# One output product of a graph network on one core: three float32r products of split operands in place of one float32 product

## The chip, the core and the metric

The kernel runs on one core of one Trainium2 chip. Its time is the device time of one execution in microseconds (us). Five engines work side by side: TensorE (PE in the profile, with PEld for its weight loads) multiplies matrices into the accumulation banks (PSUM), VectorE (DVE), ScalarE (ACT) and GpSimd (POOL) work element by element, and SyncE (SP) issues the DMAs. Each engine takes its instructions in the order in which the program put them, and waits for semaphores of the others.

## The reference

There are 128 independent graphs of 128 nodes with 256 features. Layer 0 normalizes, applies a gated graph network of three rounds (a product with a weight, a product with the adjacency matrix, a GRU cell) and adds the result to its input. Layer 1 normalizes again and applies graph attention:

```
h   = max(layernorm(x), 0)
Wh  = h W^T                               # 128 x 256 for each graph
e   = leaky_relu(s1[i] + s2[j]),  s1 = Wh a1,  s2 = Wh a2
att = softmax(e, masked by the adjacency matrix)
out = x + att Wh
```

All is float32.

## The kernel before

Four graphs make a group, and there are 32 groups (`NG`), numbered 0 to 31. A planner written in Python (class `Order`) decides, while the program is built, in which order each engine gets its instructions: every step is a generator that yields (engine, estimated length, earliest start), and the planner issues the step that can start first, with ranks that break near ties. The order is fixed in the program after that.

Layer 0 runs one round of one group at a time on TensorE and interleaves the rounds of neighbouring groups. The last round of group 30 is followed by that of group 31, which alone is done in two halves of two graphs each. Layer 1 of a group is the generator `epilogue`, started when the group's third round is done. For the last two groups it stays on the core, with no way round over DRAM. Its steps are, with the lines of the profile:

- TensorE turns the state to rows (`pr_o`, L527); DVE adds it to the input (L967), takes the statistics (L440 to L449) and POOL the inverse root; ACT normalizes (`h_b`, L471)
- DVE makes the two score columns of each graph (L998, into `s`)
- TensorE puts the mask and the turned score in a bank (`ps`, L1009 and L1016); ACT adds the other score and applies the leaky unit (`e`, L1046)
- DVE takes the row maximum (L1061, into `soft`), ACT the exponential with its sum (L1065)
- TensorE transposes the result (`pp`, L1074), ACT copies it to `prT` (L1078, or L1083 in group 31 with the scale of the normalization); DVE makes the inverse of the sum and the row scale `rs` (L1093, L1095)
- TensorE gathers the neighbours, `h` times `prT` (L637, into two banks `pq`); ACT, and for the second bank in group 31 DVE, copy them to `hs` (L1116), 128 x 1024 for the four graphs, with the features on the partitions
- TensorE makes the output product `hs` times `gwt`, the transposed weight, 128 x 256 for each graph and two products of 128 rows each (L1124); DVE multiplies it by `rs` and adds it to the rows (L1132)
- SyncE stores the rows (L60): 512 KB for a whole group, or in group 31 128 KB for each graph.

In the trace's names a bank appears as `po`, `pp`, `ps` or `pq` where it comes from the pool of three, and as `u`, `m` or `c` where, in the last stretch, one of the five banks of layer 0 is used in its place. `xt` is the tile of rows of groups 29, 30 and 31.

Of the kernel before, what the change touches and what calls it, by code (L numbers as in the profile page):

```python
# [7 lines left out]

F32 = mybir.dt.float32
I32 = mybir.dt.int32  # L10
AF = mybir.ActivationFunctionType
ALU = mybir.AluOpType
AX = mybir.AxisListType

P = 128
D = 256
C = D // P
G = 4
# [3 lines left out]
EPS = 1e-5  # L22
ALPHA = 0.2
BIG = 1e30


@with_exitstack
def preln_gnn_kernel(
# [14 lines left out]
    nc = tc.nc  # L43
    B = x.shape[0]
    NG = B // G
# [11 lines left out]
    put = on_pe  # L57
# [19 lines left out]
    small = ctx.enter_context(tc.tile_pool(name="small", bufs=4))  # L77
# [52 lines left out]
    gwt = const.tile([P, C, D], F32, name="gwt")  # L130
# [13 lines left out]
    for bank in (*c1, c2):  # L144
        bank = bank.rearrange("p g t -> p (g t)")
# [19 lines left out]
    PE, ACT, DVE, DVE2, POOL, SP = "PE", "ACT", "DVE", "DVE2", "POOL", "SP"  # L165
# [146 lines left out]
    order = Order()  # L312
# [627 lines left out]
    def epilogue(s, hT, graphs, ready):  # L940

        g = s.g
# [3 lines left out]
        name = f"{g}_{graphs[0]}"  # L946
        bank_t, row_t, graph_t = 0.57 * n / G + 0.02, 0.62 * n / G + 0.02, 0.11 * n

        late, h = g >= NG - 3, None
# [3 lines left out]
        if late:  # L953
            banks, ready = yield from to_rows(hT, ready, f"{name}_o", graphs)
        else:
            h, ready = yield from to_rows_by_blocks(hT, ready, f"b{name}")
            s.kept.append(h)
            if g < NG - XT:
                yield from load_x1(s)
                ready = max(ready, s.x1_ready)  # L960
        x1 = s.x1
        for i, two in enumerate(twos(graphs)):
            t = yield (DVE if late else DVE2), 0.31 * len(two), ready
# [8 lines left out]
        if final_one:  # L972

            rstd, nb, t, t2 = yield from norm_scales(x1, graphs, t - HOP, f"b{name}", True)
        else:
            rstd, nb, t = yield from norm_scales(x1, graphs, t - HOP, f"b{name}")
        h, t = yield from norm_apply(
            x1, graphs, None if final_one else rstd, nb, t, f"b{name}", s.kept,
            "tq" if end else "h",
        )  # L980
        if final_one:
            t = max(t, t2)
# [3 lines left out]
        ready = t  # L986
        place = min(part.start, G - 2)
        for i in (1, 0):
            for k in graphs:
                first = not late and s.prT is None  # L990
                t = yield (DVE2, 0.53, ready, "prT") if first else (DVE2, 0.53, ready)
# [12 lines left out]
        if late:  # L1004
            t = yield PE, 4 * graph_t if end else graph_t, max(t, s.off_ready), "misc"
            p2 = order.open("misc", f"ps2_{name}")
            if end:
# [3 lines left out]
                    start=True, stop=False, skip_group_check=True,  # L1011
                ))
            for k in graphs:
                turned = p2[:, k * P : (k + 1) * P]
                if end:
                    put(nc.tensor.matmul(  # L1016
                        turned, two[:, k : k + 1].to_broadcast([P, P]), ident,
                        start=False, stop=True, skip_group_check=True,
# [3 lines left out]
        else:  # L1022

            t = yield DVE, 0.1, t - HOP
            turned = score_tiles[g % 2]
            put(nc.vector.transpose(turned, turned))
            ready, line = t, None
            for q in range(Q):
                t = yield SP, 0.45, ready
# [4 lines left out]
            t = yield SP, 0.45, t + LAND, "e"  # L1034
            s.e = order.open("e", f"e_{g}")
            dma(s.e, line.rearrange("(o k) p -> o k p", o=1).to_broadcast([P, G, P]))
            t = t + 2.5
            t = t + LAND
        ready = t
        for k in graphs:  # L1040
            t = yield (ACT, 0.4, ready, e_room) if s.e is None else (ACT, 0.4, ready)
            if s.e is None:
                s.e = place_of_e(g)
            e = s.e
# [7 lines left out]
        if not end:  # L1052
            off_ready = yield from mask(s, ready)
            t = yield DVE2, row_t, max(t, off_ready) - HOP
# [3 lines left out]
        t = yield DVE, row_t, t - HOP  # L1058
        soft = small.tile([P, 4, G], F32, tag="soft", name=f"soft_{name}")
        nm, total, inv, rs = (soft[:, i, :] for i in range(4))  # L1060
        put(nc.vector.tensor_reduce(nm[:, part], le, AX.X, ALU.max, negate=True))  # L1061
        ready = t
        for k in graphs:
            t = yield ACT, 0.5, ready
# [4 lines left out]
        ready = t  # L1069
        if late:  # L1070
            t = yield PE, graph_t, t, "misc"
# [3 lines left out]
            prT = s.prT  # L1075
            if not final_one:
                t = yield ACT, bank_t, t
                put(nc.scalar.copy(prT[:, part, :].rearrange("p k s -> p (k s)"), pp[:, cols]))  # L1078
            else:
                ready = t  # L1080
                for k in graphs:
                    t = yield ACT, 0.3, ready
                    put(nc.scalar.activation(  # L1083
                        prT[:, k, :], pp[:, k * P : (k + 1) * P], AF.Identity,
                        scale=rstd[:, k : k + 1],
                    ))
            order.close(f"pp_{name}", t)
        else:
            t = yield from squares_by_blocks(e, s.prT, t, str(g))
            prT = e  # L1090
# [8 lines left out]
        banks, ready = yield from gathered(h, prT, t, f"pq_{name}", graphs)  # L1099
# [5 lines left out]
        for c, pq in enumerate(banks):  # L1105
            on = DVE if c and final_one else ACT
            t = yield (on, bank_t, ready, hs_room) if s.hs is None else (on, bank_t, ready)
            order.close(f"pq_{name}_{c}", t)
            if s.hs is None and end:
                hs = work.tile([P, 4, H], F32, tag="ta", name=f"hs_{g}")  # L1110
# [3 lines left out]
            hs = s.hs  # L1114
            copy = nc.vector.tensor_copy if on == DVE else nc.scalar.copy
            put(copy(hs[:, c, cols], pq[:, cols]))  # L1116
        ready = t

        for ks in twos(graphs) if not final_one else [range(k, k + 1) for k in graphs]:
            t = yield PE, 0.865 * len(ks), ready, "misc"  # L1120
            po = order.open("misc", f"po_{g}_{ks[0]}").rearrange("p (k d) -> p k d", d=D)
            for j, k in enumerate(ks):
                for c in range(C):
                    put(nc.tensor.matmul(  # L1124
                        po[:, j, :], hs[:, c, k * P : (k + 1) * P], gwt[:, c, :],
                        start=(c == 0), stop=(c == C - 1),
                    ))
            if final and ks[-1] == graphs[-1] and not end:
                order.close(f"hs_{g}", t)
            for j, k in enumerate(ks):  # L1130
                t2 = yield DVE, 0.4, t
                put(nc.vector.scalar_tensor_tensor(  # L1132
                    x1[:, k, :], po[:, j, :], rs[:, k : k + 1], x1[:, k, :], ALU.mult, ALU.add
                ))
            order.close(f"po_{g}_{ks[0]}", t2)
            if final_one:
                yield SP, 0.45, t2
                dma(out[g * G + k], x1[:, k, :])
        if final_one:
            return  # L1140
        t = yield SP, 0.45, t2
        ks = slice(g * G + part.start, g * G + part.stop)
# [92 lines left out]
    for slot, (g, l) in enumerate(plan):  # L1235
        s = groups[g]
# [53 lines left out]
```

## Time and profile before

| what | value |
|---|---|
| time, median of 3 runs | 2126.38 us (2125.87 to 2126.73) |
| profiled execution, first to last instruction | 2124.5 us; the profile gives no other time for it |
| granted TensorE clock over the span | 1.000 |
| TensorE busy | 2116.6 us, 10865 matmuls |
| VectorE busy | 1733.1 us |
| ScalarE busy | 1301.4 us |
| GpSimd busy | 126.5 us |
| DMA | 211.95 MB, 100 GB/s on the mean |

In the profile's rows a name such as `L1124 PE MATMUL po<-gwt,hs` is the line of the kernel, the engine, the operation and what it writes and reads. A float32 product is two matmul records. Rows of the timeline and of the chain of waits begin with the start in us from the first instruction and the length in us; `x8` are eight instructions taken together, and `[0.61 <-ACT e L1046]` says how long the engine was idle before it and what ended that. In rows of groups, busy us and the mean ns of one stand between the bars, and the idle time before them after the second bar.

### The profile page before, as it was taken

The numbers are of one execution on the slowest core, as the hardware profiler recorded it, in microseconds if no ns is written. First come the engines' busy times: TensorE is split into PE (matmuls) and PEld (weight loads), VectorE is DVE, ScalarE is ACT, GpSimd is POOL, SyncE is SP. The second block draws the span as 40 slices with busy tenths as digits, with TensorE's granted clock in tenths as the row PEclk, the third lists the DMA queues.
The fourth block names the chain that finished last, engine by engine and source line by source line (L and its number), as shares of the span: only waits on it lengthen the run. The fifth ranks groups of instructions, "written<-read, shape, count | busy, mean of one in ns | idle before, by whom it ended". The sixth has DMA issues, their size and how long they took to land.

```text
span 2124.5 us, 32340 instructions
## 1 busy us (share of the span) xinstructions
PE 2116.6 (100%) x10865; PEld 1886.8 (89%) x10865; DVE 1733.1 (82%) x3771; ACT 1301.4 (61%) x2875; POOL 126.5 (6%) x200
## 2 busy tenths in 40 slices
PE   9999999999999999999999999999999999999999
PEld 7888888888888888888888888888888888888888
DVE  7778888888878888888888888888888888787777
ACT  5556666566656666666656666666666566665666
POOL 1000000000000000000000000000000000000000
PEclk9999999999999999999999999999999999999999
DMA  5334454554455444545344554445453544444311
GB/s 159 65 85 88 86 118 107 107 117 92 98 115 119 84 96 107 122 109 113 83 108 104 117 122 82 98 106 123 110 107 88 107 107 105 96 98 94 70 31 46
DMA packets 667975, 211.95 MB, mean 100 GB/s; under 512 B 578336, under 2 KB 644640, under 8 KB 667808
## 3 DMA queue, kind: packets, MB, share of 16 engines
q1 hardware_dynamic: 667808, 209.87, 44.3%
q8 instruction: 86, 1.41, 0.3%
q14 instruction: 81, 0.66, 0.1%
HBM read 121.91 MB, written 87.88 MB: 99 GB/s over the span
## 4 chain that ended last, share of the span: by engine, by line
PE 98%; DVE 1%; ACT 0%; DMA 0%; issue 0%; POOL 0%; SPq 0%; ACTq 0%; DVEq 0%
PE c L737 35%; PE u L737 35%; PE m L737 12%; PE pa L637 8%; PE po L1124 5%; PE pq L637 2%; PE pw L378 0%; DMA xt<-in_x 0%; PE c L1124 0%; PE u L1124 0%; ACT v L688 0%; PE c L637 0%; PE pr_o L527 0%; DVE st_a L440 0%; PE pr L527 0%; ACT e L1065 0%
## 5 line engine op out<-in xcount | busy, mean ns | idle before, releaser
L830 ACT ACTIVATE z<-c,brz 128x256 f32<-128x256 f32 (+1 forms) x388 | 186.2, 480 | 328.4 <-PE c L737 186.4
L737 PE MATMUL u<-t_h,s_hh 128*128 128x256 f32 (+1 forms) x1164 | 345.0, 378 | 0.9 <-DVE c L763 0.5
L737 PE MATMUL u<-t_a,s_f 128*128 128x256 f32 (+1 forms) x1164 | 312.3, 377 | 0.0
L737 PE MATMUL c<-aT,s_f 128*128 128x256 f32 (+1 forms) x1164 | 312.3, 377 | 0.0
L795 ACT ACTIVATE r<-c,brz 128x256 f32<-128x256 f32 (+1 forms) x388 | 175.3, 475 | 194.3 <-PE c L737 112.8
L763 DVE TENSOR_TENSOR c<-u,m 128x512 f32<-128x512 f32 (+1 forms) x194 | 134.6, 694 | 140.8 <-PE u L737 140.4
L737 PEld LDWEIGHTS u<-t_h,s_hh 128*128 128x128 f32 x1164 | 218.4, 190 | 31.3 <-ACT c L757 1.6
L737 PEld LDWEIGHTS c<-aT,s_f 128*128 128x128 f32 x1164 | 220.4, 190 | 28.9
L737 PEld LDWEIGHTS u<-t_a,s_f 128*128 128x128 f32 x1164 | 220.4, 190 | 29.0
L737 PE MATMUL c<-hT,s_hh 128*128 128x256 f32 (+1 forms) x780 | 229.8, 376 | 0.0
L837 DVE TENSOR_TENSOR v<-v,c 128x256 f32<-128x256 f32 (+1 forms) x388 | 153.6, 415 | 66.3 <-PE c L737 43.7
L770 ACT COPY c<-u 128x512 f32<-128x512 f32 (+1 forms) x194 | 109.7, 566 | 117.5 <-PE u L737 116.1
L760 ACT COPY m<-m 128x512 f32<-128x512 f32 (+1 forms) x194 | 112.7, 581 | 107.1 <-PE m L737 106.9
L802 ACT ACTIVATE v<-c,bhn 128x256 f32<-128x256 f32 (+1 forms) x388 | 173.0, 474 | 0.0
L737 PE MATMUL m<-t_h,s_hh 128*128 128x256 f32 (+1 forms) x582 | 172.3, 378 | 0.0
L737 PE MATMUL c<-t_h,s_hh 128*128 128x256 f32 (+1 forms) x582 | 172.1, 377 | 0.0
L737 PEld LDWEIGHTS c<-hT,s_hh 128*128 128x128 f32 x780 | 147.6, 190 | 19.2
L774 DVE TENSOR_TENSOR c<-u,m 128x512 f32<-128x512 f32 (+1 forms) x194 | 131.8, 679 | 37.9 <-ACT c L770 34.9
L737 PE MATMUL u<-aT,s_f 128*128 128x256 f32 (+1 forms) x582 | 156.2, 377 | 0.0
L737 PE MATMUL m<-t_a,s_f 128*128 128x256 f32 (+1 forms) x582 | 156.1, 377 | 0.0
L737 PE MATMUL c<-t_a,s_f 128*128 128x256 f32 (+1 forms) x582 | 156.1, 377 | 0.0
L757 ACT COPY c<-u 128x512 f32<-128x512 f32 (+1 forms) x194 | 109.8, 566 | 43.7 <-PE u L737 43.7
(164 smaller groups left out, 3928.4 us busy)
## 6 DMA issues: line engine op xcount, KB each, us to landing
z<-tq SPq DMA_DIRECT2D x248, 128.0 KB
h<-z SPq DMA_DIRECT2D x248, 128.0 KB
xt<-in_x SPq DMA_DIRECT2D x31, 512.0 KB
z_a<-tq_a SPq DMA_DIRECT2D x120, 128.0 KB
hT_a<-z_a SPq DMA_DIRECT2D x120, 128.0 KB
z_b<-tq_b SPq DMA_DIRECT2D x116, 128.0 KB
h_b<-z_b SPq DMA_DIRECT2D x116, 128.0 KB
x<-in_x SPq DMA_DIRECT2D x29, 512.0 KB
```

The costliest lines, as they stand in the source:

```text
L637: put(nc.tensor.matmul(pa[:, k * P : (k + 1) * P], h[:, k, c * P : (c + 1) * P], A[:, k, :], start=True, stop=True,))
L737: put(nc.tensor.matmul(to(q), S[0][:, gate_no, weight, :], moving, start=first and q == 0 and i == 0, stop=(i == len(ends) - 1), skip_grou ...
L757: put(nc.scalar.copy(c1[0][:, :, 0:W], u[:, :, 0:W]))
L760: put(nc.scalar.copy(m[:, :, 0:W], m7[:, :, 0:W]))
L763: put(nc.vector.tensor_tensor(c2[:, :, 0:W], u[:, :, 0:W], m[:, :, 0:W], ALU.add))
L770: put(nc.scalar.copy(c1[1][:, :, 0:W], u[:, :, 0:W]))
L774: put(nc.vector.tensor_tensor(c22[:, :, 0:W], u[:, :, 0:W], m[:, :, 0:W], ALU.add))
L795: put(nc.scalar.activation(r[:, o, cols], src, AF.Tanh, bias=brz[:, o : o + 1], scale=0.5))
L802: put(nc.scalar.activation(v[:, o, cols], src, AF.Identity, bias=bhn[:, o : o + 1], scale=0.5))
L830: put(nc.scalar.activation(z[:, o, cols], src, AF.Tanh, bias=brz[:, C + o : C + o + 1], scale=0.5))
L837: put(nc.vector.tensor_tensor(v[:, o, cols], v[:, o, cols], src, ALU.add))
L1124: put(nc.tensor.matmul(po[:, j, :], hs[:, c, k * P : (k + 1) * P], gwt[:, c, :], start=(c == 0), stop=(c == C - 1),))
```

## The change

For group 30 alone (`g == NG - 2`) the output product is made otherwise. The operand `hs` is split into a part `hi` (ACT, `hs` times a factor just below one, written as float32r), the rest `lo` (DVE, `hs - hi`) and a combination `dif` (DVE). The weight `gwt` is split in the same way into `ghi` (ACT), `glo` and `gdif` (DVE, three steps). These six take three buffers of the pool `h`, two of `prT` and one of `e`. The product is then hi times ghi plus lo times glo in one bank, and dif times gdif in a second bank; each is multiplied by its own row scale (`rs_more`, `rs`) and added to the rows, so that there are two adds for each graph. The steps of the planner after that, the store among them, are unchanged.

```diff
+        halves = None
+        if g == NG - 2:
+            planes = []
+            t = ready
+            for i in range(3):
+                t = yield DVE, 0.1, t, "h"
+                planes.append(order.open("h", f"po_{g}_{i}").rearrange("p g d -> p (g d)").rearrange("p (c t) -> p c t", c=C).bitcast(F32R))
+            hi, lo, dif = planes
+            t = yield ACT, 1.2, t
+            put(nc.scalar.activation(hi, hs, AF.Copy, scale=BELOW))
+            t = yield DVE2, 1.22, t
+            put(nc.vector.tensor_tensor(lo, hs, hi.bitcast(F32), ALU.subtract))
+            t = yield DVE2, 1.22, t
+            put(nc.vector.scalar_tensor_tensor(dif, lo.bitcast(F32), -1.0 / UNIT, hi.bitcast(F32), ALU.mult, ALU.add))
+            ready = t
+            wides = []
...
+            t = yield ACT, 0.7, t
+            put(nc.scalar.activation(ghi, gwt, AF.Copy, scale=BELOW))
+            t = yield DVE2, 0.7, t
+            put(nc.vector.tensor_tensor(gdif, gwt, ghi.bitcast(F32), ALU.subtract))
+            t = yield DVE, 0.4, t
+            put(nc.vector.tensor_scalar(glo, gdif.bitcast(F32), 1.0 / UNIT, None, ALU.mult))
+            t = yield DVE2, 0.7, t
+            put(nc.vector.scalar_tensor_tensor(gdif, ghi.bitcast(F32), -UNIT, gdif.bitcast(F32), ALU.mult, ALU.add))
+            t = yield DVE, 0.1, t
+            rs_more = small.tile([P, 4, G], F32, tag="soft", name=f"more_{g}")[:, 0, :]
+            put(nc.vector.tensor_scalar(rs_more, rs, 1.0 + UNIT, None, ALU.mult))
+            halves = (hi, ghi), (lo, glo), (dif, gdif)
+            ready = max(ready, t)
...
+            if halves is not None:
+                for j, k in enumerate(ks):
+                    for c in range(C):
+                        for X, W in halves[:2]:
+                            put(nc.tensor.matmul(
+                                po[:, j, :], X[:, c, k * P : (k + 1) * P], W[:, c, :],
+                                start=(c == 0 and X is halves[0][0]), stop=(c == C - 1 and X is halves[1][0]),
+                            ))
+                t = yield PE, 0.5, t, "misc"
+                po2 = order.open("misc", f"po2_{g}_{ks[0]}").rearrange("p (k d) -> p k d", d=D)
+                X, W = halves[2]
+                for j, k in enumerate(ks):
+                    for c in range(C):
+                        put(nc.tensor.matmul(
+                            po2[:, j, :], X[:, c, k * P : (k + 1) * P], W[:, c, :],
+                            start=(c == 0), stop=(c == C - 1),
+                        ))
+                for j, k in enumerate(ks):
+                    for bank, scales_ in ((po, rs_more), (po2, rs)):
+                        t2 = yield DVE, 0.4, t
+                        put(nc.vector.scalar_tensor_tensor(
+                            x1[:, k, :], bank[:, j, :], scales_[:, k : k + 1], x1[:, k, :], ALU.mult, ALU.add
+                        ))
...
+                continue
```

The constants are `BELOW = 1 - 2^-13` and `UNIT = 2^-12`.

## The prediction

> **What bounds the kernel now.** The page first: TensorE is busy throughout and is 98% of the chain of waits.
>
> ```profile
> span 2124.5 us, 32340 instructions
> ...
> PE 98%; DVE 1%; ACT 0%; DMA 0%; issue 0%; POOL 0%; SPq 0%; ACTq 0%; DVEq 0%
> ```
>
> The change touches group 30 alone (NG is 32). Comparing the two built programs engine by engine, every queue is the same up to some 12 us before the end; what differs is the tail, so only the tail is priced. Second view: the chain of waits in order of time, from 2105 us on.
>
> ```profile
> 2111.06 1.73 PE po L1124 x8
> 2112.78 0.22 PE pp L1074 x2
> ...
> 2113.88 1.73 PE u L1124 x8
> 2115.61 0.45 PE m L637 x4
> ...
> 2117.72 0.89 PE pq L637 x8
> ...
> 2120.34 0.88 PE m L1124 x4
> 2121.22 0.02 issue
> 2121.24 0.48 DVE xt L1132
> ```
>
> `po` at 2111.06 and `u` at 2113.88 are group 30's output product: 16 matmul records in 3.46 us, each float32 product of 256 columns being two records 0.216 us apart. They stand between steps of group 31's softmax (`pp` transposes, `m` and `pq` gather), whose last add ends at 2121.72. Third view: the timeline of the tail, for what the other engines do there.
>
> ```profile
> 2112.35 9.74 SPq L60 DMA_DIRECT2D out<-xt  x6
> ...
> 2113.10 0.62 ACT L1083 ACTIVATE prT<-pp,norm_b 128x128 f32<-128x128 f32 x2 [1.75 <-PE pp L1074]
> 2113.92 0.62 ACT L1046 ACTIVATE e<-ps,s 128x128 f32<-128x128 f32 x2 [0.20 <-PE ps L1016]
> 2114.57 0.42 DVE L1061 TENSOR_REDUCE soft<-e 128x2 f32<-128x256 f32 x1 [0.61 <-ACT e L1046]
> 2115.03 0.40 ACT L1065 ACTIVATE e<-e,soft 128x128 f32<-128x128 f32 x1 [0.49 <-DVE soft L1061]
> ...
> 2121.24 0.48 DVE L1132 SCALAR_TENSOR_TENSOR xt<-m,soft,xt 128x256 f32<-128x256 f32 x1 [0.38 <-PE m L1124]
> ```
>
> The row to keep in mind is the maximum `L1061` of group 31's second half: it starts the moment its scores `e` are there, ACT's exponentials start 0.46 us later, and all that follows hangs on it: 7.15 us from its start (2114.57) to the last add's end (2121.72). Fourth view: the groups by form, VectorE (DVE) and ScalarE (ACT), for the prices.
>
> ```profile
> L694 DVE TENSOR_TENSOR hT<-hT,v 128x1024 f32<-128x1024 f32 x7 | 8.5, 1221 | 4.1 <-ACT v L688 4.1
> L698 DVE SCALAR_TENSOR_TENSOR hT<-hT,v 128x1024 f32<-128x1024 f32 x9 | 10.9, 1216 | 0.1
> L1055 DVE TENSOR_TENSOR e<-e,A 128x512 f32<-128x512 f32 x4 | 2.8, 690 | 0.2
> L930 DVE TENSOR_SCALAR A<-A 128x512 f32<-128x512 f32 x6 | 2.5, 415 | 0.0
> L1132 DVE SCALAR_TENSOR_TENSOR xt<-u,soft,xt 128x256 f32<-128x256 f32 x3 | 1.4, 480 | 1.0 <-PE u L1124 1.0
> L688 ACT ACTIVATE v<-v,bih 128x512 f32<-128x512 f32 x8 | 5.3, 715 | 0.0
> ```
>
> **The change, part by part.** The sum is made on this execution: span 2124.5 us; the median of the runs, 2126.38, is 1.88 us more, carried over unchanged.
>
> *Removed.* 16 records x 0.216 = 3.46 us of PE in front of group 31. `pp` then waits only for ACT's second exponential, whose accumulator is read by 2111.35, so `prT` runs at 2111.85 instead of 2113.10: 1.25 us earlier.
>
> *First split, on ACT and DVE.* In the new queues ACT's `hi` (128x1024) stands right behind `prT`: 715 ns for 512 columns, 499 ns for 256 (same line), so 0.22 us per 256 and 1.15 us for 1024: 2112.40 to 2113.55. Behind it wait `e` of group 31's second half and an `hs` copy; `e` is complete at 2114.36, against 2114.54 before, so the head start is spent. On DVE the queue is: `lo` (1.22 us, waiting for `hi`) to 2114.8, group 31's `hs` copy (0.42) to 2115.15, `dif` (1.22) to 2116.3, one add (pitch 0.40), then `L1061`. It starts at 2116.60 where it stood at 2114.57: **2.03 us later**, though its input was ready at 2114.36. This wait is the first cost, and PE and ACT idle for it.
>
> *From there to group 31's last add.* The chain of 7.15 us repeats with small shifts. On ACT `ghi` (0.71) comes between the exponentials and `prT` while PE transposes: 0.1 late. On DVE `gdif`, `glo` and `gdif` again (0.69 + 0.42 + 0.69) stand ahead of the last `hs` copy, which waits 0.44 us for them (ready 2120.0, done 2120.86). On PE eight float32r matmuls stand between group 31's last two products. Walked through with the rows, the `hs` copy ends 4.26 us after the maximum instead of 4.50 (PE's queue is emptier), and the last add 2.92 us after that instead of 2.65 (the eight matmuls, 0.89, less a product that is done by then): 2123.78, 7.18 us after the maximum. So **+0.03**.
>
> *The adds of group 30* now come last in DVE's queue: eight of 128x256 where there were four in the middle. Two independent ones together take 0.88 us in the timeline (at 2112.82), so 0.40 apart; dependent steps stand their duration plus 0.05 apart (`hT` at 2088.63, 2089.38 and 2090.11, 0.69 to 0.72 long), so 0.53; with four dependent pairs they end 3.75 us after group 31's last: **+3.75**. PE is ahead of them by then: at 0.111 us per float32r matmul its last is done at 2125.
>
> *The last transfer.* SyncE's queue now ends with group 30's 512 KB instead of 128 KB of group 31. The issue at 2112.35 (third view) has moved its 512 KB by 2114.93; the last 128 KB issue, at 2121.75, by 2123.10. That is 2.58 against 1.35 us: **+1.24**, with nothing left to hide it. The four 128 KB stores move ahead of it into an idle queue at no cost.
>
> *Pace of float32r.* No row has one. The built program has one matmul instruction for each (24 in place of 16). Low end: 0.111 us, two records of 128 columns (`pq`, 8 in 0.89 us). High end: 0.433, a whole float32 product. Between them, 0.216: the same columns at a float32 record's pace. I take 0.111, by the row that is nearest in kind, another type with one record to a product: the three bfloat16 products at the start (L146) pass 512 columns in about 0.42 us, where float32 records pass 256 in 0.426 in the same stretch, so such a record is twice as fast. 0.216 is kept as a rival.
> The Trainium skill, "FP8 and Floating Point Precision" (TensorE Precision Notes), says that true float32 takes four passes through the array, and reduced-precision float32 is read and truncated. By that one pass would be an estimated 0.433/4 = 0.108 us, and the sum the same within 0.05 us; the two records per product agree with multiple passes but do not show four.
>
> Sum: 2.03 + 0.03 + 3.75 + 1.24 = 7.05, so a span of 2131.5 and a time of **2133.4 us** (+0.33%).
>
> *Bounds of the rest.* `hi`: 0.99 (from copies, 586 and 372 ns) to 1.43 (twice 715): -0.16 to +0.28. The splits on DVE, writing float32r: at the rate of the `L930` row 0.8 us each for `lo` and `dif`, -1.2 with the weight's part, of which only the 0.44 us of waiting lies on the path; `glo` at 0.69 instead of 0.42: +0.27. Adds: all at 0.40, -0.5; all at 0.53 with a wait, +0.5. I take the rows of the same shape; the ends stay in the range. Planes and weights go into buffers whose readers were done over 10 us before (group 29's `e` is transposed at 2084), and opening them issues nothing: no cost, and if such a wait existed it would lengthen the first split one to one.
>
> *A rule against the change.* In the tail PE will have holes of up to 1.6 us (2113.6 to 2115.2, 2116.6 to 2118). This trace shows the granted clock at 1.00 to the end, also where PE is busy only 3.14 of 4.00 us (2104 to 2108); at the very start 256-column float32 records were 0.426 us apart instead of 0.216. I take full pace.
> "TensorE: Matmul & The Clock Gate" (The HAM clock gate) says that about 3.4 us of idleness halve the clock. No hole is that long; if the sparse stretch counted, rival 2's second case would hold.
>
> **Rivals.**
> 1. *float32r at the pace of a float32 record, 0.216 us.* The eight matmuls in front of group 31's last product take 1.73 instead of 0.89: +0.84; the last four records of group 30 then end at 2127.5 and its adds wait 0.6 us for them. 2134.9 us. For: every float32 record of 256 columns here takes that, and float32r has as many bytes. Against: float32's records come in pairs, and the bfloat16 row.
> 2. *The product is no cheaper than float32, 0.433 us, or the clock falls.* PE ends at 2132.6 and three adds follow: span 2138.2, time 2140.1; or, at half pace as in the start-up row, the 3.3 us of matmuls on the path after 2117 (`pp` 0.22, `pq` 0.89, products 1.30, eight float32r 0.89) double: 2136.7. For: nothing in the tail's rows. Against: the granted clock above.
> 3. *Not slower: the maximum is not held.* Group 31 comes forward by the PE time taken away. With no split in front of it `L1061` would start 0.8 us after `prT`, at 2113.25, 3.35 us before my 2116.60, and the sum fall to +3.7: 2130.1, within 0.2% of before. It decides where the maximum starts by 2113.8: `hi`, `lo`, the copy, `dif` and one add, 4.4 us by the rows, would have to take 1.6. Against: their order is fixed by the program, and three of them have rows over 1.1 us. Faster would need the eight adds and the 512 KB to be hidden as well, and nothing comes after them.
>
> **How the numbers follow.** Forecast (one pass, maximum held) 0.62; rival 1 0.2; rival 2 0.1; rival 3 0.05; something else 0.03. 0.2% of the time, 4.3 us, is about what a measurement of this kernel can tell from no change. All but rival 3 lie above 2130.6; slower 0.94, same 0.04, faster 0.02. Range: the low bounds together (-0.16 - 1.2 - 0.5) give 2131.5, and half a us of the way to rival 3 2131.0; the high ones (+0.28 + 0.27 + 0.5) on rival 1 give 2136.0, with part of rival 2 2137.0.
>
> **What would show it.** `L1061`'s second-half maximum starting about 2 us after its `e`, behind two 1.22 us rows; float32r records about 0.11 us apart; eight adds ending DVE's queue near 2127.5; a 512 KB store ending the span about 4 us later. Wrong if DVE's float32r rows are far from the float32 ones, if the records are 0.2 us or more apart, or if a new wait holds the planes.

## The result, and the profile after

| | before | after |
|---|---|---|
| time, median | 2126.43 us (2125.57 to 2127.82, 6 executions) | 2133.32 us (2132.89 to 2133.47, 6 executions) |
| profiled execution: its time, its span | 2126.38, 2124.5 us | 2133.34, 2131.6 us |
| ratio to before | | 1.0032, 95% interval 1.002 to 1.0044 |

The change makes the kernel 6.9 us slower; 2133.4 was forecast, with a range of 2131.0 to 2137.0. On the page of the changed kernel, the span and the shares of the chain of waits by engine read:

```profile
span 2131.6 us, 32379 instructions
...
PE 98%; DVE 1%; ACT 1%; issue 0%; DMA 0%; SPq 0%; DVEq 0%; ACTq 0%
```

These shares are those of before within 1%: a tail of some 20 us does not show in them. The timeline of the tail does (start, length, engine, line; the lines are 3 further on than before in the steps that were there, and L1132, once the add, is now the split `lo`; the adds are L1196 and, in group 30, L1180):

```profile
2112.21 1.05 ACT L1130 ACTIVATE po<-hs 128x1024 fp32r<-128x1024 f32 x1
2112.48 15.47 SPq L63 DMA_DIRECT2D out<-xt  x6
...
2113.29 1.23 DVE L1132 TENSOR_TENSOR po<-hs,po 128x1024 fp32r<-128x1024 f32 x1 [0.85 <-ACT po L1130]
...
2114.44 0.42 DVE L1119 COPY hs<-u 128x256 f32<-128x256 f32 x1
2114.77 1.22 DVE L1134 SCALAR_TENSOR_TENSOR po<-po,po 128x1024 fp32r<-128x1024 f32 x1
...
2115.90 0.48 DVE L1196 SCALAR_TENSOR_TENSOR xt<-m,soft,xt 128x256 f32<-128x256 f32 x1
2116.30 0.41 DVE L1064 TENSOR_REDUCE soft<-e 128x2 f32<-128x256 f32 x1
...
2116.74 0.40 ACT L1068 ACTIVATE e<-e,soft 128x128 f32<-128x128 f32 x1 [2.69 <-DVE soft L1064]
...
2120.22 0.42 DVE L1119 COPY hs<-pq 128x256 f32<-128x256 f32 x1
...
2121.04 1.30 PE L1164 MATMUL po<-w,po 128*128 128x256 f32 x8
...
2122.18 1.03 PE L1188 MATMUL u<-gwt,hs 128*128 128x256 f32 x4
...
2123.25 0.48 DVE L1196 SCALAR_TENSOR_TENSOR xt<-u,soft,xt 128x256 f32<-128x256 f32 x1 [1.33 <-PE u L1188]
...
2127.06 0.48 DVE L1180 SCALAR_TENSOR_TENSOR xt<-c,soft,xt 128x256 f32<-128x256 f32 x1
```

From the top: `hi` on ACT, then on DVE without a gap `lo`, a copy, `dif`, an add, and only then the maximum L1064, for which ACT had been idle 2.69 us. Group 31's last add ends at 2123.73, the eight adds of group 30 at 2127.54, and the 512 KB store ends the span.

**How the runs are compared.** The profiled executions do not reach the tail at the same moment: group 31's first-half maximum, ahead of everything that the change touches, starts between 2108.9 and 2110.8 us. The difference is there from the first microseconds (the 31st matmul record starts at 13.0 us in the kernel before, at 13.2 in the one after and at 14.9 in the latest run, e9) and is carried through. The rows of the start-up show where it arises, first in the kernel before, then in e9:

```profile
5.20 6.71 PE L378 MATMUL pw<-wih,wt 128*128 128x256 f32 x14 [0.16 <-DMA wih<-in_w_ih_t]
```

```profile
5.84 7.92 PE L379 MATMUL pw<-wih,wt 128*128 128x256 f32 x14 [0.62 <-DMA wih<-in_w_ih_t]
```

The same 14 float32 matmuls start 0.64 us later, behind a load, and take 1.21 us more. The last of them have 512 columns; in e9 they start 0.85 us apart up to 11.1 us and 0.43 apart from 11.9 on, while before the 0.43 begins at 8.7. A factor of two is what a halved clock gives in e7 further down (float32 records of 256 columns 0.43 us apart instead of 0.216), so the moment at which the clock rises seems to be the larger part of the start-up difference. All stages below are counted from the start of the first-half maximum, which takes the start-up out; it is probably also why the executions of one kernel scatter by 1 to 2 us.

| us from the first-half maximum | second-half maximum starts | group 31's last add ends | last add ends | span ends |
|---|---|---|---|---|
| before | 5.52 | 12.67 | 12.67 | 15.49 |
| after | 7.38 | 14.82 | 18.62 | 22.65 |
| e1, late split | 4.25 | 11.31 | 18.48 | 22.51 |
| e12, late split, hole filled | 4.25 | 11.31 | 17.44 | 21.47 |
| e2, store by graph | 7.38 | 14.82 | 18.63 | 21.25 |
| e3, no third product | 7.13 | 14.20 | 15.76 | 19.80 |
| e4, planes as float32 | 7.38 | 17.32 | 25.19 | 29.21 |
| e5, no weight split on DVE | 7.39 | 14.36 | 18.17 | 22.19 |
| e8, weight first, planes late, store by graph | 5.23 | 12.19 | 16.25 | 18.86 |
| e7, hi times ghi alone | 6.49 | 14.55 | 16.12 | 20.14 |
| e6, float32, moved late | 4.25 | 12.06 | 14.18 | 18.21 |
| e9, one float32r product in place | 4.37 | 11.15 | 11.15 | 13.97 |

The change costs 22.65 - 15.49 = 7.16 us, in four pieces: the maximum 1.86 later; 7.44 instead of 7.15 from there to group 31's last add, 0.29; 3.80 for the adds behind it; and 4.03 instead of 2.82 from the last add to the end, 1.21.

### The profile page after: what moved, and what is told of

It is laid out like the page before. It is cut to its first block, busy times and chain, and to the rows that moved or that the text cites. A ratio compares the mean times of both kernels' runs of the same rounds, so it can differ in the third digit from the quotient of the medians.

```text
span 2131.6 us, 32379 instructions
## 1 busy us (share of the span) xinstructions
PE 2117.8 (99%) x10873; PEld 1883.2 (88%) x10873; DVE 1738.7 (82%) x3781; ACT 1303.5 (61%) x2877; POOL 126.6 (6%) x200
## 4 chain that ended last, share of the span: by engine, by line
PE 98%; DVE 1%; ACT 1%; issue 0%; DMA 0%; SPq 0%; DVEq 0%; ACTq 0%
PE c L740 35%; PE u L740 35%; PE m L740 11%; PE pa L640 8%; PE po L1188 5%; PE pq L640 2%; PE pw L381 1%; DVE xt L1180 0%; DMA wih<-in_w_ih_t 0%; DVE prT L1001 0%; ACT v L691 0%; PE pr_o L530 0%; ACT e L1068 0%; PE pr L530 0%; DVE t_h L496 0%
```

## The experiments

Seven edits of the changed kernel come first (e1, e12, e2, e3, e4, e5, e8), then the cheaper product and the move by themselves (e7, e6, e9), then the product in all groups. The six split operands are called planes. Their type, float32r, has 32-bit words like float32, but a product of 256 columns is one matmul record of 0.12 us in the changed kernel, where float32 has two of 0.216.

**e1: the splits behind the maximum**

```diff
             planes = []
-            t = ready
+            t = ready + 4.0
```

> The whole change stays; only the planner's earliest start of the first split is set 4 us later, so that in the fixed order hi stands behind prT of group 31's second half on ACT, and lo and dif behind its row maximum on DVE. Theory (the maximum is held by the splits in front of it on DVE, and what is held there comes back later because DVE must still do the same work): the maximum starts at about 2114.0 instead of 2116.30, group 31's last products come forward by about as much, but the splits and the eight adds follow one another on DVE; walked through with the rows, the last add ends at about 2126.4 instead of 2127.54, so a span of 2130.5 (-1.1 us). Rival A (the held maximum alone is the loss of 2 us): -1.9 us or more, a span of 2129.7 or less. Rival B (DVE is not what ends the tail): no change, 2131.6.

Measured: 2133.22 us, ratio 1.0031 (1.0019 to 1.0042). The maximum starts 3.13 us earlier and group 31's last add ends 3.51 earlier, yet the last add ends only 0.14 earlier. The theory's 1.1 us is missing, and the windows of the late-split kernel show where it went (the windows are cut at the clock's own steps; columns: us, busy us and instructions of PE, PEld, DVE, ACT and POOL, then the granted clock, the DMA share and GB/s):

```profile
2118.12:2121.54 3.42, 1.06 (x7) 0.71 (x5) 3.35 (x7) 0.00 (x0) 0.00 (x0) 1.00 0.24 81
2121.54:2124.95 3.41, 3.41 (x18) 3.41 (x18) 2.02 (x6) 0.00 (x0) 0.00 (x0) 0.50 0.00 0
2124.95:2128.36 3.41, 0.87 (x7) 0.66 (x6) 2.19 (x5) 0.00 (x0) 0.00 (x0) 1.00 0.01 2
```

and its timeline, TensorE's rows:

```profile
2121.31 1.70 PE L1164 MATMUL u<-w,po 128*128 128x256 f32 x7 [2.36 <-DVE w L1148]
```

In the fixed order the second float32r record needs `lo` and `glo`, and DVE now makes `glo` late, behind `lo`, `dif`, `gdif` and two adds: TensorE waits 2.36 us for it, and then runs at half its clock for 3.41 us (its float32r records stand 0.213 us apart instead of 0.12). Neither the theory nor a rival had that.

**e12: the same, with TensorE kept busy in the hole**

```diff
             if halves is not None:
+                if ks[0] == 0:
+                    for _ in range(6):
+                        put(nc.tensor.matmul(po[:, 0, :], hs[:, 0, 0:P], gwt[:, 0, :], start=True, stop=True))
```

> The late-split kernel (first split 4 us later) with one edit: six float32 products, whose result is overwritten, stand on TensorE just ahead of group 30's first float32r product, in the 2.36 us in which TensorE waited for the weight's low part there and after which its granted clock was 0.50 for 3.41 us. Nothing else moves. Theory (the lack of work in that stretch halved the clock, and the half clock took back most of what the late split had gained): the clock stays at 1.00, the seven records behind the wait stand 0.12 us apart instead of 0.213, and the last add ends 17.5 us after the start of the first-half maximum instead of 18.48; span 2130.4 (-1.0 us), although there is more work. The Trainium skill, TensorE: Matmul & The Clock Gate (The HAM clock gate), ties the half clock to the last free-running window of about 3.4 us having been idle, and would have the same outcome. Rival (the clock falls for another reason, so that the extra 2.6 us of products only cost): no change or slower, 2131.4 to 2132.

Measured: 2133.19 us, ratio 1.0029 (1.0018 to 1.0041). The windows of the same stretch, again 3.41 us each, and the timeline's row behind the hole:

```profile
2119.82:2123.23 3.41, 3.41 (x20) 3.06 (x19) 3.32 (x6) 0.00 (x0) 0.00 (x0) 1.00 0.24 80
2123.23:2126.64 3.41, 2.24 (x19) 2.04 (x17) 2.80 (x7) 0.00 (x0) 0.00 (x0) 1.00 0.00 0
```

```profile
2122.22 1.33 PE L1167 MATMUL u<-w,po 128*128 128x256 f32 x8
```

The clock stays at 1.00; eight records now take less than seven did. Group 31's last add is where it was in e1 (11.31), the last add ends 1.04 us earlier (17.44; 17.5 was expected) and so does the tail. So the half clock came from the lack of work, it cost 1 us, and with 2.6 us more products the tail is shorter. (At the spacing of 3.41 us the hole would have lain inside one window here too, 2119.82 to 2123.23, as it did in e1; a different position of the windows does not explain it.) With the hole filled e1's theory holds as it stood: 18.62 - 17.44 = 1.18 us, against 1.1. The two medians are equal all the same, and the span is 2131.5 where 2130.4 was expected: this execution reached the tail 1.14 us later, and 1 us is inside the scatter of the start-up. The gain rests on the stages of one profiled execution of each kernel, not on the times.

**e2: the last store in four**

```diff
                             x1[:, k, :], bank[:, j, :], scales_[:, k : k + 1], x1[:, k, :], ALU.mult, ALU.add
                         ))
+                    yield SP, 0.45, t2
+                    dma(out[g * G + k], x1[:, k, :])
...
-        if final_one:
+        if final_one or halves is not None:
             return
```

> The whole change stays; the only edit is on SyncE's queue: group 30's 512 KB store becomes four stores of 128 KB, each behind the last add of its graph. Theory (the last store's size is on the path in full): the last add ends where it did, 2127.54, and the span ends 2.8 us after it instead of 4.0, at 2130.3 (-1.2 us). Rival (what follows the last add is a fixed cost of any store, not its bytes): no change, 2131.6.

Measured: 2132.46 us, ratio 1.0028 (1.0017 to 1.0039). The last add ends at 18.63 as before; from there to the end it is 2.62 us instead of 4.03, so -1.40 (-1.2 expected). The term of the store was about as large as forecast, and it can be taken back without touching the rest.

**e3: without the third product**

```diff
-            put(nc.vector.scalar_tensor_tensor(dif, lo.bitcast(F32), -1.0 / UNIT, hi.bitcast(F32), ALU.mult, ALU.add))
...
-            put(nc.vector.scalar_tensor_tensor(gdif, ghi.bitcast(F32), -UNIT, gdif.bitcast(F32), ALU.mult, ALU.add))
...
-                        put(nc.tensor.matmul(
-                            po2[:, j, :], X[:, c, k * P : (k + 1) * P], W[:, c, :],
-                            start=(c == 0), stop=(c == C - 1),
-                        ))
...
                         t2 = yield DVE, 0.4, t
-                        put(nc.vector.scalar_tensor_tensor(
+                        if bank is po:
+                            put(nc.vector.scalar_tensor_tensor(
```

> The order of everything that remains is that of the changed kernel. Left out are dif, the second gdif, the third product (dif times gdif) and its four adds, so that the output of group 30 lacks that part. Theory (DVE in order): without dif the next thing late is the add behind group 31's product m, whose operand copy waits for lo; so the maximum starts at about 2115.8 instead of 2116.30 (-0.5, not the -1.2 of the removed instruction); the last hs copy no longer waits for gdif (-0.45); four adds end the queue instead of eight (-2.1). Last add at 2124.5, span 2128.5 (-3.1 us). Rival A (the removed DVE time counts in full: 1.22 + 0.69 + 4 x 0.48): -3.8 us, span 2127.8, the maximum at 2115.1. Rival B (the splits and adds are hidden beside PE's products): a span within 0.5 us of 2131.6.

Measured: 2131.07 us, ratio 1.0020 (1.0011 to 1.0029). The tail is 2.85 us shorter (3.1 by the theory, 3.8 by rival A). Timeline of this kernel:

```profile
2115.54 0.70 PE L1184 MATMUL m<-gwt,hs 128*128 128x256 f32 x2 [0.37 <-DVE hs L1119]
...
2116.28 0.48 DVE L1192 SCALAR_TENSOR_TENSOR xt<-m,soft,xt 128x256 f32<-128x256 f32 x1 [0.79 <-PE m L1184]
2116.68 0.41 DVE L1064 TENSOR_REDUCE soft<-e 128x2 f32<-128x256 f32 x1
```

Taking 1.22 us of `dif` from DVE moves the maximum by only 0.25: the add in front of it now waits 0.79 us for product `m`, whose operand copy stands behind `lo`. Two chains held the maximum, a quarter of a us apart, and removing one shows the other.

**e4: the same planes read as float32**

```diff
-            halves = (hi, ghi), (lo, glo), (dif, gdif)
+            halves = [(a.bitcast(F32), b.bitcast(F32)) for a, b in ((hi, ghi), (lo, glo), (dif, gdif))]
```

> Every instruction stays in its place; the 24 products read the same six planes as float32 instead of float32r. Theory (a float32r product is one record of 0.12 us against two of 0.216 us, and eight of them stand in front of group 31's last product): the maximum stays at 2116.30, group 31's last add moves from 2123.73 to about 2126.1, and group 30's last products end at about 2132.4, so that the last three adds wait for them; last add at 2133.9, span 2137.9 (+6.3 us). Rival A (PE has enough room, only what stands in front of group 31's last add counts): +2.4 us, span 2134.0. Rival B (float32r is no faster than float32 in kind, and the records only look short): no change, 2131.6.

Measured: 2141.13 us, ratio 1.0068 (1.0053 to 1.0083). The tail is 6.56 us longer than after the change. Timeline:

```profile
2122.09 3.62 PE L1164 MATMUL po<-w,po 128*128 128x256 f32 x16
...
2126.61 0.48 DVE L1196 SCALAR_TENSOR_TENSOR xt<-u,soft,xt 128x256 f32<-128x256 f32 x1 [3.83 <-PE u L1188]
```

The eight products in front of group 31's last one are 16 records, and group 31's last add ends 2.50 us later (2.4 expected); the rest comes from the products that its successors wait for. This is what float32r saves in the changed kernel: on this path its type is worth 6.6 us, and even so the change as a whole loses 7.2.

**e5: without the weight's split on DVE**

```diff
-            put(nc.vector.tensor_tensor(gdif, gwt, ghi.bitcast(F32), ALU.subtract))
...
-            put(nc.vector.tensor_scalar(glo, gdif.bitcast(F32), 1.0 / UNIT, None, ALU.mult))
...
-            put(nc.vector.scalar_tensor_tensor(gdif, ghi.bitcast(F32), -UNIT, gdif.bitcast(F32), ALU.mult, ALU.add))
...
-            halves = (hi, ghi), (lo, glo), (dif, gdif)
+            halves = (hi, ghi), (lo, ghi), (dif, ghi)
```

> The changed kernel with the three DVE steps of the weight's split (gdif, glo, gdif) left out; all three products take ghi as their weight, so the output of group 30 differs by the small parts of the weight. Theory (of the weight's split only the wait of the last hs copy lies on the path, 0.47 us in the profile after): the maximum stays at 2116.30, the copy starts at about 2119.75 instead of 2120.22, group 31's last add ends at 2123.26, the last add at 2127.07, span 2131.1 (-0.5 us); the rest of the excess between the maximum and group 31's last add (7.43 against the 7.18 forecast) stays. Rival A (the weight's split is what makes that stretch long, beyond the copy's wait): -0.75 us or more. Rival B (it is hidden): no change, 2131.6.

Since the third product takes `ghi` in the place of `gdif` as well, more than the weight's small parts differ. Measured: 2133.29 us, ratio 1.0032 (1.0019 to 1.0045); the start-up hides the gain in the times. By the stages the maximum stays (7.39) and group 31's last add, the last add and the end each come 0.46 us earlier: 1.81 us of DVE work were worth the one wait of the `hs` copy. From the maximum to group 31's last add it is then 6.97 us; the excess over the forecast stays, so it isn't the weight's.

**e8: the best order found for the whole change**

The block of the weight's four steps is moved ahead of the block of `hi`, `lo` and `dif`, and the stores are those of e2; besides that:

```diff
+            t = ready
             wides = []
...
             planes = []
-            t = ready
+            t = max(t, ready + 4.0)
```

> The whole change stays, exact as it is, in another order: the weight's split (ghi, gdif, glo, gdif) comes first, in the gaps of ACT and DVE before and around the maximum; hi, lo and dif come 4 us later, behind group 31's last exponentials and hs copies; and the 512 KB store is four stores of 128 KB. This puts the weight's split where the late-split kernel let PE wait for it. Theory (what the change costs is DVE's queue, 5.5 us of splits and 3.8 of adds, of which an order can hide only what fits into DVE's gaps before the last product): the maximum starts at about 2114.6 instead of 2116.30, the last add ends at 2125.6 instead of 2127.54, the stores save 1.2 to 1.4, span 2128.4 (-3.2 us), still 3.9 us over the kernel before. No hole of PE is over 1 us, so the granted clock stays 1.00. Rival A (a good order hides the splits: only the adds and the store stay): a span of 2126.5 or less. Rival B (no gain from order, as the late-split kernel had none; only the stores count): 2130.3.

Measured: 2129.80 us, ratio 1.0015 (1.0005 to 1.0024). Timeline of this kernel:

```profile
2114.36 0.41 DVE L1064 TENSOR_REDUCE soft<-e 128x2 f32<-128x256 f32 x1
2114.69 0.68 DVE L1138 SCALAR_TENSOR_TENSOR w<-w,w 128x512 fp32r<-128x512 f32 x1
...
2118.19 1.22 DVE L1148 TENSOR_TENSOR po<-hs,po 128x1024 fp32r<-128x1024 f32 x1
...
2119.72 1.22 DVE L1150 SCALAR_TENSOR_TENSOR po<-po,po 128x1024 fp32r<-128x1024 f32 x1
```

The tail is 3.79 us shorter than after the change (3.2 expected) and 3.37 longer than before. Group 31 is now earlier than in the kernel before (12.19 against 12.67): the whole remaining loss stands behind it, 4.06 us to the last of group 30's adds. Rival A falls (the span is 2128.0 and not 2126.5 or less: the order hides the splits from group 31, but nothing hides the adds), rival B too (order is worth 2.4 us beside the stores).

**e7: hi times ghi alone**

The edits of e3 and the weight's three steps of e5, and in addition:

```diff
-            put(nc.vector.tensor_tensor(lo, hs, hi.bitcast(F32), ALU.subtract))
...
-                        for X, W in halves[:2]:
+                        for X, W in halves[:1]:
...
-                    for bank, scales_ in ((po, rs_more), (po2, rs)):
+                    for bank, scales_ in ((po, rs), (po2, rs)):
```

> The changed kernel with hi times ghi alone: lo, dif, glo, both gdif, two of the three products and four of the eight adds are left out, so group 30's output is that of one float32r product. The order of what remains is that of the changed kernel. Theory: the maximum now waits only for the add behind product m, 2115.2 instead of 2116.30; from there to group 31's last add about 6.6 us (no weight split in front of the hs copy, four float32r matmuls instead of eight in front of the last product); four adds of 0.40 us and the 512 KB store follow: last add at 2123.5, span 2127.5, still 3 us over the kernel before though the product itself takes 1 us instead of 3.5. Rival A (without the splits the cheaper product is a gain): a span below 2124.5. Rival B (the splits cost nothing): 2131.6 less the four adds, 2129.5 or more.

Measured: 2130.30 us, ratio 1.0019 (1.0009 to 1.0029). The maximum starts at 6.49 (6.3 expected, the add behind `m` being what holds it). Eight of the ten executions lie at 2129.8 to 2130.7, near the theory's span of 2127.5 plus the 1.9 by which times exceed spans; two, the profiled one among them, at 2132.5 and 2132.6, with a mean clock of 0.998 where the others have 0.999 or 1.000. The windows of the profiled one:

```profile
2117.37:2120.78 3.41, 2.25 (x12) 1.51 (x12) 1.18 (x5) 2.35 (x8) 0.00 (x0) 1.00 0.22 77
2120.78:2124.19 3.41, 3.41 (x11) 2.83 (x11) 0.77 (x3) 0.00 (x0) 0.00 (x0) 0.50 0.11 39
```

Here too the clock was halved for one window of 3.41 us, in which group 31's last products stand: from the maximum to group 31's last add it took 8.06 us where 6.6 was expected, which is why the row of e7 in the table is long. Half of 3.41, 1.7 us, is the most that the clock can have cost; these two executions lie 2.4 us above the middle of the others (2130.2), and the rest may be start-up, since this one reached the first-half maximum late, at 2110.63. With a full clock, too, this kernel is some 3.4 us slower than before, with a product that is cheaper and no low parts at all.

**e6: the float32 product, only moved**

```diff
-        ready = t
+        ready = t + (8.0 if g == NG - 2 else 0.0)
```

> The kernel before, with float32 products and no split at all; only the planner's earliest start of group 30's output product is set 8 us later, so that these products stand among group 31's last ones, four adds and the 512 KB store come last. Theory (moving the product behind group 31 costs the adds and the larger store, but gives back part of the PE time in front of group 31; the loss of the change is mostly in the splits): the maximum starts at about 2113.2 instead of 2114.57, the last add ends at about 2122.2 instead of 2121.72, the store takes 1.2 us more, span 2126.2 (+1.7 us over the kernel before). Rival A (the move to the end is the loss, the splits are not): +4 to +5 us, span 2129 or more. Rival B (order makes no difference, the work is what counts): 2124.5.

Measured: 2129.85 us, ratio 1.0014 (1.0005 to 1.0023). The tail is 2.72 us longer than before, 1.51 up to the last add and 1.21 behind it: between the theory's 1.7 and rival A's 4 to 5, nearer to the theory. Timeline:

```profile
2114.29 0.42 DVE L1061 TENSOR_REDUCE soft<-e 128x2 f32<-128x256 f32 x1 [0.72 <-ACT e L1046]
...
2117.78 2.93 PE L1124 MATMUL po<-gwt,hs 128*128 128x256 f32 x12
...
2120.55 1.03 PE L1124 MATMUL u<-gwt,hs 128*128 128x256 f32 x4
...
2121.41 1.89 PE L1124 MATMUL m<-gwt,hs 128*128 128x256 f32 x8
...
2123.34 0.88 DVE L1132 SCALAR_TENSOR_TENSOR xt<-m,soft,xt 128x256 f32<-128x256 f32 x2 [1.24 <-PE m L1124]
```

TensorE works from 2117.78 to the last add without a gap; my walk had put the end of it 1 us too early. So the place alone, without any split, costs 2.72 us with the float32 product. The other 4.4 of the change's 7.16 us are a net: the splits, the doubled adds and their order, less what the cheaper product gives back there.

**e9: one float32r product at the old place**

The float32r copy of the weight is made where `e` of group 30 is opened:

```diff
+            put(nc.gpsimd.tensor_copy(rounded[0], gwt))
...
-            hs = s.hs
+            hs = s.hs.bitcast(F32R) if g == NG - 2 else s.hs
...
-                        po[:, j, :], hs[:, c, k * P : (k + 1) * P], gwt[:, c, :],
+                        po[:, j, :], hs[:, c, k * P : (k + 1) * P], (rounded[0] if g == NG - 2 else gwt)[:, c, :],
```

> The kernel before, in its own order, with one change: ACT writes group 30's hs as float32r, GpSimd makes a float32r copy of the weight 10 us ahead, and the output product is one float32r product at its old place, so that group 30's output has the precision of float32r. Theory (only the first half of the product, 1.73 us, stood in front of the chain of group 31; the second half was beside it): po takes 0.48 us, prT starts at about 2111.85 and the maximum at 2113.3 instead of 2114.57, the chain of 7.15 us follows: last add 2120.4, span 2123.2 (-1.3 us against the kernel before). Rival A (PE is 98% of the chain, so all of the saved 2.5 us comes off): span 2122.0. Rival B (the second exponential or GpSimd's copy holds the chain): 2124.5 or more.

Measured: 2125.51 us beside 2126.78 for the kernel before, ratio 0.9995 (0.9986 to 1.0005), not to be told from no change by the times. By the stages the tail is 1.52 us shorter (1.3 by the theory, 2.5 by rival A):

```profile
2112.46 0.93 PE L1132 MATMUL po<-gr,hs 128*128 128x256 f32 x4
...
2114.25 0.72 PE L1132 MATMUL u<-gr,hs 128*128 128x256 f32 x4
```

Only the first of the two stood in front of group 31's chain: the maximum comes 1.15 us earlier, and the chain behind it gains the other 0.37. This is what a cheaper product gives at this place in this order, with nothing to pay for the split.

**e10 and e11: one float32r product in all 32 groups**

```diff
-    gwt = const.tile([P, C, D], F32, name="gwt")
-    dma(gwt, gat_w_t.rearrange("(c p) o -> p c o", p=P))
+    gwt = const.tile([P, C, D], F32R, name="gwt")
+    gwt_in = io.tile([P, G, D], F32, tag="x1", name="gwt_in", bufs=2)[:, 0:C, :]
+    dma(gwt_in, gat_w_t.rearrange("(c p) o -> p c o", p=P))
...
+        if g == 0:
+            put(nc.gpsimd.tensor_copy(gwt, gwt_in))
...
-            hs = s.hs
+            hs = s.hs.bitcast(F32R)
```

and in e11 also:

```diff
-            t = yield PE, 0.865 * len(ks), ready, "misc"
+            t = yield PE, 0.6 * len(ks), ready, "misc"
```

> The kernel before, in its own order on every engine, with the output product of all 32 groups as one float32r product (hs written as float32r by the copies that are there, the weight rounded once at the start), so that the whole output has the precision of float32r in this product. Theory (the tail hides a cheaper product, the body does not, because PE is busy throughout there): each group saves 16 x 0.216 - 8 x 0.12 = 2.5 us of PE; 31 groups stand in the body, so -70 to -80 us, a time near 2052 us; ACT and DVE, at 61% and 82% of the span, have room for it. Rival A (the order, planned for the longer product, makes PE wait for DVE instead): -20 to -50 us. Rival B (a cheaper product is worth as little in the body as in the tail): under 5 us.

> The kernel with one float32r output product in all 32 groups, with the planner told 0.60 us a graph for that product instead of 0.865 (it measures 0.33), so that all steps may be ordered anew. Theory (of the 24 us in which PE is idle there, some 14 are waits for DVE that an order planned for the shorter product avoids): 5 to 12 us less than 2073.2. Rival (DVE has no more to give in the recurrent rounds, whatever the order): within 2 us of 2073.2, either way.

Measured: e10 2073.16 us, ratio 0.9747 (0.9731 to 0.9763); e11 2058.81 us, ratio 0.9682 (0.9666 to 0.9698). Groups of TensorE by line: the product before, then in e10, then what stands in front of the recurrent rounds in e10 and in e11 (behind the second bar, TensorE's idle time and its cause).

```profile
L1124 PE MATMUL po<-gwt,hs 128*128 128x256 f32 x484 | 114.5, 379 | 0.0
```

```profile
L1128 PE MATMUL po<-gwt,hs 128*128 128x256 f32 x242 | 49.7, 326 | 0.1
...
L739 PE MATMUL u<-t_h,s_hh 128*128 128x256 f32 (+1 forms) x1164 | 348.1, 381 | 13.3 <-DVE c L765 12.6 <-ACT c L759 0.6
```

```profile
L739 PE MATMUL u<-t_h,s_hh 128*128 128x256 f32 (+1 forms) x1164 | 344.9, 378 | 0.8 <-DVE c L765 0.5 <-ACT c L759 0.2
```

Half the records, and the busy time of the group falls from 114.5 to 49.7 us. That is 65 us, short of the theory's 70 to 80, but the row misleads: the first float32r record of a group of four starts 0.03 us behind the start of the last float32 record and 0.305 ahead of its own successor, 0.333 together, which is 0.216 for the float32 record and 0.118 for the float32r one. From the start of the last float32 record to the start of the next one behind the four it is 0.68 to 0.70 us, 0.216 and four times 0.118 to 0.12. TensorE's busy time as a whole says the same; it was 2116.6 us before and 2047.5 in e10, and in e11 the page has:

```profile
PE 2041.0 (99%) x10609; PEld 1818.5 (88%) x10609; DVE 1717.2 (84%) x3771; ACT 1297.7 (63%) x2875; POOL 120.5 (6%) x201
```

That is 75.6 us less than before, as the theory had it. e10's 53.5 us fall between the theory and rival A: TensorE's idle time in the span rose from 7.9 to 24.3 us, 13.3 of it in front of L739 and 12.6 of these for DVE's L765, in an order planned for the longer product. e11 shows that it was the order: these waits are gone (13.3 to 0.8), and the time falls by another 14.4 us, more than the 5 to 12 expected. These two kernels are faster than both kernels of this study, but they are another trade: their output product has float32r's precision, which the change spent its splits to avoid.

## Why the prediction was right

- *The bound and the place.* Right: what the change costs stands in the tail, and ahead of it the profiles differ by the start-up.
- *The held maximum, +2.03.* Measured 1.86. `hi` took 1.05 us where 1.15 was taken from three rows of other widths; the queue behind it ran as listed. e1 shows that the splits hold it (it starts 3.13 earlier with them behind it), and e3 that `dif` is not alone in that.
- *From there to the last add, +0.03.* The one term that was mis-sized by more than 0.2: 0.29. The `hs` copy's wait was as forecast (0.46 by e5, 0.44 predicted), and the copy ended 4.34 us after the maximum, at 2120.64, where the walk had 4.26. From there to the last add's end it took 3.09 us where the walk had 2.92. The two float32 records that had waited for the copy (2120.69 to 2121.23) took 0.54 instead of 0.43, since the first stands 0.32 ahead of the second. The eight float32r matmuls, costed at 0.89 us, took 0.95 behind them (to 2122.18), 0.119 each instead of 0.111. With the copy's 0.08 that is 0.25 of the 0.26.
- *The adds, +3.75.* Measured 3.80; with half of them (e3) it is 1.56. They are what stays in every order of the change that was tried.
- *The last transfer, +1.24.* Measured 1.21; e2 takes back 1.40.
- *The sum.* 7.05 against 7.16. It is closer than its parts, because the first two terms are off by -0.17 and +0.26; and that the median lies within 0.1 us of the forecast is partly luck, since six executions of the kernel before alone spread over 2 us.
- *The pace.* One record to a product, 0.12 us, near the low bound as chosen. e4 sets the price of being wrong: 6.56 us for full float32, where rival 2's first case had 6.7. The Trainium skill, FP8 and Floating Point Precision (TensorE Precision Notes), counts four passes for true float32. A quarter of the measured 0.433 us is an estimated 0.108; the record has 0.12, and that decides.
- *The full clock.* Right for the changed kernel (1.00 up to 2128 us), but not for the reason given. No hole is 3.4 us long there, and none ahead of the last product is in e1 either, where the clock was halved; that it stayed up here was in part luck. Rival 2's second case was closer than its share of a chance of 0.1 says: a half clock came in e1, in two of ten executions of e7, and in e10 and e11. It cost 1.0 us in e1 and at most 1.7 in the others, where that rival had 3.3.
- *Rival 3* would have needed the maximum at 2113.8 or earlier. Of the kernels with all the splits only the late ones, e1 and e12, do that (4.25 us behind the first-half maximum, 2113.14 in e1), and the adds and splits then follow at the end: the tail stays 7.0 us longer than before, or 6.0 with the hole filled, where rival 3 had 3.7. That rival overlooked that the work in front of the maximum is only moved, to where nothing hides it.

## What to carry to other kernels

A cheaper product is worth what waits for it: in the body, where TensorE is the chain, a single float32r product gave 54 us over 32 groups and 68 once the order was planned for its real length, while in the tail it gave 1.5, and with the splits that are to keep its precision it cost 7. Before adding steps to an in-order engine, list what is queued behind them there; taking one away shows the next chain a quarter of a microsecond behind it. Where runs differ by a start-up of 2 us, count the stages from an event ahead of the change.

## What was not expected of the hardware

- **The clock is halved without a long hole.** In e1 it falls after a window of 3.42 us in which TensorE was busy 1.06 us (longest wait 2.36 us), and the steps of the clock stand at 2121.54, 2124.95 and 2128.36, each 3.41 us on; in e7 at 2120.78 and 2124.19. It also falls for one such window near the end of e10 and of e11, after windows with 1.42 and 1.30 us of busy rows. The Trainium skill, TensorE: Matmul & The Clock Gate (The HAM clock gate), has a free-running window of 3413 ns, which fits; it speaks of an idle window, and these were partly busy. Where the limit lies stays open. By the same spacing the changed kernel had a window with 2.03 us of busy rows (2115.11 to 2118.53) and e3 one with 1.64 (2122.53 to 2125.94), and both kept their clock; e7's had 2.25 and did not, in two executions of ten. So the busy share of the window does not decide by itself; the position of the windows may, but that was not tried.
- **A float32r record behind float32 ones looks longer than it is.** It starts 0.03 us behind the start of the last 256-column float32 record and 0.304 to 0.308 ahead of its own successor, in the changed kernel as in nearly all groups of e10. Together that is 0.216 + 0.12: the switch of type itself costs nothing that these rows show, but sums of busy time by line move some 0.19 us from one line to the other.
- **Writing float32r costs DVE and ACT nothing extra here**: the splits of 128x1024 on DVE took 1225 and 1216 ns, against 1221 and 1216 for the same operations in float32 before; ACT's copies of 128x512 to `hs` took 583 ns as float32r in e10, against 582 as float32 before.
